# Layer 1's feed-forward norm: one pass over four batches, or each batch behind its own end

## The chip, the cores and the metric

The kernel runs on one core of a Trainium2 chip, as one program. The metric is the device time of one execution in microseconds (us). The core's engines work side by side, each through its own list of instructions in order: TensorE (PE in the profile: matrix products and transposes; PEld is its loading of weights), VectorE (DVE), ScalarE (ACT), GpSimd (POOL) and SyncE (SP). SP, ACT and POOL also start DMA transfers. An instruction that waits for a semaphore holds up everything behind it on its engine.

## The reference

A transformer of four layers works on x of 4 batches with 256 tokens of 256 features. Each layer is a cross attention (`xattn`) and a feed-forward part (`ffn`), both on a layer norm of x and both added to x. The stretch that matters is layer 1, between the end of layer 0's feed-forward and layer 1's experts:

```python
x = x + _L0_ffn_ref(_layernorm(x), ...)        # 32 experts, the best 8 of each token
x = x + _L1_xattn_ref(_layernorm(x), ...)
x = x + _L1_ffn_ref(_layernorm(x), ...)

def _L1_xattn_ref(Z, kv, ...):
    ...                                         # summary: one row of 256 for each batch, from kv alone
    y = Z + summary
    return (y - mu) / jnp.sqrt(var + LN_EPS) * gamma + beta

def _L1_ffn_ref(X, gate_w, router_bias, W1, W3, W2, sw1, sw3, sw2):
    scores = jax.nn.sigmoid(X @ gate_w.T)       # 8 experts
    _, idx = jax.lax.top_k(scores + router_bias, 2)
    ...
    y = jnp.einsum('eth,ehd->etd', jax.nn.silu(h1) * h3, W2)
    shared = (jax.nn.silu(X @ sw1.T) * (X @ sw3.T)) @ sw2.T
    return jnp.einsum('etd,te->td', y, gate_full) + shared
```

So layer 1's attention is for each batch a norm, an added row, a second norm, a scale and a shift: no matrix product on tokens. Its feed-forward part needs the third norm of the same batch, for the routing scores, for a shared expert that all tokens pass, and for the experts.

## The kernel before

A batch is one tile `x[b]` of [128, 2, 256]: token q*128+p lies in partition p. Everything is f32.

**Adding layer 0's experts (`l0_add`, L632 to L668).** For each of 8 token tiles t, GpSimd issues eight indirect gathers `f0yt` (L655), one for each of the eight chosen experts, into a ring of 24 buffers; two tiles later VectorE adds them to x (L647, eight instructions, whose order against each other is pinned). After every second tile a batch is whole, and `l1_xattn(b)` (L1303) runs on it: layer norm to y, plus the summary (L1308), layer norm to z, gamma (L1312), beta (L1313), added to x (L1314). All of this is VectorE's, save the roots of the norms, which ScalarE takes.

**Work for later in between (`fill`, L178).** Beside this, TensorE makes keys and values of the context for layer 2. That is a generator, `l2_early` (L1316); `fill(n)` takes n steps of it. A unit of it has 7 product steps (L1351: four matmuls 128x256 into PSUM, names `fill`, `filly`, `fillg`, `fillt` by buffer, copied by ScalarE to `kr_early`, L1358, and `va_early`, L1359, with squares, L1369, and sums of them on VectorE, L1370), a scaling of `kr_early` (L1376, by the engine in `self.scaler`) and 4 turn steps (L1385: transposes, copied by ScalarE to `kT_early`, L1387). `l0_add` takes `G0 = 9` steps for each t. What is left of the generator when layer 2 begins is taken there, at once.

**Layer 1's feed-forward (`l1_ffn`, L800).** It begins with `normed` (L188), which for each of the four batches in turn makes a layer norm `xn` (L152 to L163: stats L156, aggregate L157, root L125, reciprocal L126, scaled and shifted L160), stores it to DRAM as `f1xd` from ScalarE's queue (L195), takes `F1 = [1, 2, 2, 3]` steps of `fill`, turns it with four transposes `tp_ln` (L202) and copies them to `xnT` by turns on VectorE (L112) and ScalarE (L114). Then come 16 small products for the routing logits, the sigmoid (`l_sc`, L878), the choice of two experts (`first`, `l_sel` on), a table of slots, gathers from `f1xd`, and 23 expert tiles with `G1` fill steps between them. Beside the routing runs `shared_expert`, a generator of steps: each computes two pairs of products `f1gu` of a token tile, silu of one half on ScalarE (L831), times the other half on VectorE (L832), transposes `f1tps` and products `f1y`. All `f1gu`, the logits too, share two PSUM buffers.

**Order.** A scheduler places the instructions of each engine by their estimated readiness; `pin` (and `ordered`) fix one instruction's place behind the pinned one before it on the same engine. So lines of the program can change place against each other unless they are pinned or depend on each other. ScalarE's functions live in tables: root, sigmoid and silu are in different ones, and an `ACT_TABLE_LOAD` stands in its list wherever the next function needs another.

Of the kernel before, what the change touches and what calls it, by code (L numbers as in the profile page):

```python
# [11 lines left out]
F32 = mybir.dt.float32  # L12
# [6 lines left out]
AF = mybir.ActivationFunctionType  # L19
# [5 lines left out]
P = 128  # L25
B = 4
S = 256
NT = B * S
D = 256
# [10 lines left out]
E1, I1, SH1, K1 = 8, 176, 352, 2  # L40
# [7 lines left out]
F0 = [0, 0, 0, 0, 2, 12, 4, 4]  # L48
G0 = 9
REGS = 4  # L50
F1 = [1, 2, 2, 3]
G1 = [7, 4, 4, 3, 2, 2, 2, 2, 2, 2, 0]
LN2, Q2, C2 = 2, 2, 6
FIRST3 = [7, 1, 3]
# [43 lines left out]
class Kernel:  # L98
# [47 lines left out]
            if k < 2:  # L146
                yield 0.9

    def layernorm(self, out, x):

        nc = self.nc
        st = self.small.tile([P, 2, 6], F32, name="ln_st")  # L152
        mv = self.small.tile([P, 2, 2], F32, name="ln_mv")
        rs = self.small.tile([P, 2], F32, name="ln_rs")
        for q in range(2):
            nc.vector.bn_stats(st[:, q, :], x[:, q, :])  # L156
            nc.vector.bn_aggr(mv[:, q, :], st[:, q, :])  # L157
        self.rstd(rs, mv[:, :, 1], 1.0, self.eps5)
        for q in range(2):
            nc.vector.tensor_scalar(  # L160
                out[:, q, :], x[:, q, :], mv[:, q, 0:1], rs[:, q : q + 1],
                ALU.subtract, ALU.mult,
            )  # L163
# [469 lines left out]
    def l0_add(self, two, weights):  # L633


        nc = self.nc
        slot, gate, yd = self.back0
        self.scaler = nc.vector
        take = self.take
        self.take = self.wide_take  # L640
        rows = []

        def add(t):
            xt = self.x[t // 2][:, t % 2, :]
            for r in range(K0):
                self.pin(
                    nc.vector.scalar_tensor_tensor(xt, rows.pop(0), gate[:, t, r : r + 1], xt, ALU.mult, ALU.add)  # L647
                )
            if t % 2:
                self.l1_xattn(t // 2)  # L650

        for t in range(9):
            for r in range(K0 if t < 8 else 0):
                yt = two.tile([P, D], F32, name="f0yt", bufs=3 * K0)
                nc.gpsimd.indirect_dma_start(  # L655
                    out=yt, out_offset=None, in_=yd[:, :],
                    in_offset=bass.IndirectOffsetOnAxis(ap=slot[:, t, r : r + 1], axis=0),
                )
                rows.append(yt)
            if t > 1:  # L660
                add(t - 2)
            self.fill(G0)
            if t > 5:
                next(weights, None)
        add(7)
        self.idle(self.take()[:, :D], self.y1[:, 0, :], 4)
        self.scaler = nc.gpsimd
        self.take = take  # L668
# [128 lines left out]
    def l1_ffn(self, weights):  # L797
# [7 lines left out]
        nc, tc = self.nc, self.tc  # L805
# [3 lines left out]
        with ExitStack() as es:  # L809
            one = es.enter_context(tc.tile_pool(name="f1one", bufs=1))  # L810
            two = es.enter_context(tc.tile_pool(name="f1two", bufs=2))
            ps, ps_g, ps_y = self.psf
            s13, s2, w13, w2 = self.w1f
            for _ in weights:
                pass
            xd = self.dram.tile([NT, D], F32, name="f1xd")
            yd = self.dram.tile([NS * P, D], F32, name="f1yd")

            slot = one.tile([P, K1, 8], U32, name="f1slot")
# [2 lines left out]
            ei = one.tile([1, NS], U32, name="f1ei")  # L822
            rt = es.enter_context(tc.tile_pool(name="f1r", bufs=1))
            low, keep, lane, tok = self.low, self.keep[:, :E1], self.lane, self.tok
            xT = self.normed(ps, F1[:B], xd, rt)

            def gated(gu, w, x, h):

                for k in range(2):
                    self.mm(gu, x(k), w(k), k == 0, k == 1)  # L830
                nc.scalar.activation(h, gu[:, :I1], AF.Silu)  # L831
                nc.vector.tensor_tensor(h, h, gu[:, I1:], ALU.mult)  # L832

            def products():
                return ps_g.tile([P, 512], F32, name="f1gu", tag="gu")

            def shared_expert():

                last = None
                for t in range(9):  # L840
                    now = None
                    if t < 8:
                        h = two.tile([P, SH1], F32, name="f1hs")
                        for c in range(2):
                            gated(
                                products()[:, : 2 * I1], lambda k: s13[:, c, k, :],
                                lambda k: xT[t // 4][:, k, (t % 4) * P : (t % 4 + 1) * P], h[:, c * I1 : (c + 1) * I1],
                            )
                        now = (t, h)
                    if last is not None:  # L850
                        u, h = last
                        tp = ps.tile([P, 3, P], F32, name="f1tps", tag="tp")
                        hT = two.tile([P, 3, P], F32, name="f1hTs")
                        y = ps_y.tile([P, 512], F32, name="f1y", tag="y")[:, :D]
                        for m in range(3):
                            n = min(P, SH1 - m * P)
                            nc.tensor.transpose(tp[:n, m, :], h[:, m * P : m * P + n], self.ident)
                        nc.scalar.copy(hT[:, :2, :], tp[:, :2, :])
                        nc.scalar.copy(hT[:n, 2, :], tp[:n, 2, :])
                        for m in range(3):  # L860
                            n = min(P, SH1 - m * P)
                            self.mm(y, hT[:n, m, :], s2[:n, m, :], m == 0, m == 2)
                        xt = self.x[u // 2][:, u % 2, :]
                        nc.vector.tensor_tensor(xt, xt, y, ALU.add)
                    last = now
                    yield

            shared = shared_expert()
            beside = lambda n: [next(shared, None) for _ in range(n)]

# [42 lines left out]
            for n in range(NS):  # L913
                t = two.tile([P, D], F32, name="f1xr", bufs=4)
                nc.gpsimd.indirect_dma_start(
                    out=t, out_offset=None, in_=xd[:, :],
# [39 lines left out]
            def through(n):  # L956
                h = two.tile([P, I1], F32, name="f1h", bufs=3)
                gated(
                    products()[:, : 2 * I1], lambda k: w13[:, bass.ds(expert[n], 1), k, :],
                    lambda k: xsT[n][:, k, :], h,  # L960
                )
                return h
# [32 lines left out]
            for t in range(11):  # L995
                for r in range(K1 if t < 8 else 0):
                    yt = two.tile([P, D], F32, name="f1yt", bufs=4 * K1)
                    nc.gpsimd.indirect_dma_start(
                        out=yt, out_offset=None, in_=yd[:, :],
# [304 lines left out]
    def l1_xattn(self, b):  # L1304
        nc, one, rows = self.nc, self.a1, self.rows1
        y = one.tile([P, 2, D], F32, name="y1", bufs=2)
        self.layernorm(y, self.x[b])
        nc.vector.tensor_tensor(y, y, self.summary[b][:, None, :].to_broadcast([P, 2, D]), ALU.add)  # L1308
        self.y1 = y
        z = one.tile([P, 2, D], F32, name="z1", bufs=2)  # L1310
        self.layernorm(z, y)
        nc.vector.tensor_tensor(z, z, rows["l1_gamma"][:, None, :].to_broadcast([P, 2, D]), ALU.mult)  # L1312
        nc.vector.tensor_tensor(z, z, rows["l1_beta"][:, None, :].to_broadcast([P, 2, D]), ALU.add)  # L1313
        nc.vector.tensor_tensor(self.x[b], self.x[b], z, ALU.add)  # L1314

    def l2_early(self, ctxT):  # L1316

# [1347 lines left out]
```

## Time and profile before

| | |
|---|---|
| time, median of 3 runs | 2369.67 us (2365.74 to 2370.74) |
| the profiled execution | 2363.93 us |
| its span (first to last instruction) | 2362.2 us |
| mean granted TensorE clock | 0.981 |
| `l0_add` in the span | about 372 to 504 us |
| layer 1's feed-forward up to the first expert tile | about 504 to 552 us |
| its expert tiles | about 552 to 640 us |

PE is busy 96% of the whole span and DVE 62%, but these shares average over stages with different limits; the stretch of the change is read by windows. A row of the profile's groups has the line, the engine, the operation, `out<-in` by the names above with partitions x elements, then how often, busy time and the mean of one. These are the norm's and the turn's operations on VectorE from 457 to 520 us:

```profile
L156 DVE BATCH_NORM_STATS2 ln_st<-x 128x6 f32<-128x256 f32 x12 | 4.8, 408 | 0.0
L157 DVE BATCH_NORM_AGGREGATE ln_mv<-ln_st 128x2 f32<-128x6 f32 x18 | 2.9, 169 | 0.1
L160 DVE TENSOR_SCALAR xn<-x,ln_mv,ln_rs 128x256 f32<-128x256 f32 x8 | 2.8, 404 | 0.2
L112 DVE COPY xnT<-tp_ln 128x512 f32<-128x512 f32 x2 | 1.4, 693 | 1.5 <-PE tp_ln L202 1.5
```

The first line reads: twelve instructions of L156, 4.8 us in all, 408 ns each, with no idle time of VectorE ahead of them. In the last, 1.5 us of idle time lay ahead of the two copies, ended by the transposes. Lines of a timeline begin with the start in the span and the length; what stands in brackets is the idle time of that engine just before and what ended it.

### The profile page before, as it was taken

To read this page: it belongs to the slowest core of one execution; us is meant where nothing else is said; L and a number is where in the kernel's file an instruction comes from. 1 tells how busy PE (TensorE), PEld (TensorE's weight loads), DVE (VectorE), ACT (ScalarE), POOL (GpSimd) and SP (SyncE) were. 2 spreads that over 40 slices of the span, in tenths; PEclk is the share of its full clock that TensorE was granted. 3 is DMA by queue.
4 is the path that set the end of the run, shared out by engine and by line. 5 is a ranking of instruction groups with operands and counts; after the bars stand their busy time and mean duration, and the time that the engine had idled before them with its cause. 6 is when DMAs were issued, how large, how long until landed. Compare 5 with 4: busy or idle time off the path is not lost.

```text
span 2362.2 us, 42374 instructions
## 1 busy us (share of the span) xinstructions
PE 2256.3 (96%) x14395; PEld 1383.5 (59%) x14395; DVE 1464.7 (62%) x3534; ACT 1271.0 (54%) x2884; POOL 944.4 (40%) x1716
## 2 busy tenths in 40 slices
PE   8999997889989999999999999999999989999998
PEld 5677876767745555555555565555765633343332
DVE  5553532783557777877787777877434484748343
ACT  3334443552474555555555555554332488888996
POOL 2015655503345544555545555444212253424220
PEclk9999998999999999999999999999899999999999
DMA  7165575652551111111111111100434354434320
GB/s 270 42 203 175 173 152 157 198 182 72 166 179 40 36 51 46 53 52 51 52 56 51 52 43 51 43 24 10 193 126 114 89 169 120 107 100 104 81 68 18
DMA packets 157166, 234.47 MB, mean 99 GB/s; under 512 B 33993, under 2 KB 122825, under 8 KB 155754
## 3 DMA queue, kind: packets, MB, share of 16 engines
q1 hardware_dynamic: 140902, 190.86, 25.1%
q0 software_dynamic: 11280, 31.60, 5.4%
q10 hardware_dynamic: 4772, 9.31, 1.3%
q8 instruction: 118, 1.93, 0.3%
q14 instruction: 94, 0.77, 0.1%
HBM read 169.94 MB, written 61.74 MB: 98 GB/s over the span
## 4 chain that ended last, share of the span: by engine, by line
PE 80%; DVE 8%; DMA 3%; issue 3%; ACT 2%; POOL 2%; SPq 0%; ACTq 0%; DVEq 0%; another core or an unknown queue 0%; POOLq 0%
PE o L117 18%; PE s L117 17%; PE o L77 7%; PE b L77 4%; PE f2gu L117 3%; PE s L77 3%; PE fill L1351 3%; PE acc L117 2%; PE f1gu L117 2%; PE tpq L117 2%; PE f0gu L117 2%; PE av L117 2%; DMA f0xr<-f0xd,f0src 2%; PE f0y L117 1%; PE f2y L117 1%
## 5 line engine op out<-in xcount | busy, mean ns | idle before, releaser
L1616 ACT ACTIVATE p<-s,nmsm 128x448 f32<-128x448 f32 (+2 forms) x512 | 324.4, 638 | 388.3 <-DVE nmsm L1611 316.8
L117 PE MATMUL o<-pT,va 128*128 128x256 f32 (+2 forms) x1920 | 431.7, 377 | 0.4 <-DVE pT L1660 0.3
L117 PE MATMUL s<-kT,qT 128*32 128x448 f32 (+2 forms) x4096 | 424.2, 550 | 4.2 <-ACT p L1616 4.2
L77 ACT ACTIVATE e<-s 128x1024 f32<-128x1024 f32 (+1 forms) x416 | 392.9, 1040 | 54.3 <-PE s L77 53.1
L117 PEld LDWEIGHTS o<-pT,va 128*128 128x128 f32 (+1 forms) x1920 | 344.8, 190 | 124.7 <-issue 72.5
L1654 POOL TENSOR_SCALAR p<-p,rm 128x416 f32<-128x416 f32 x508 | 317.0, 645 | 6.3
L1611 DVE TENSOR_REDUCE nmsm<-s 128x1 f32<-128x448 f32 (+4 forms) x384 | 293.1, 784 | 4.2
L1660 DVE STREAM_TRANSPOSE pT<-p 128x448 f32<-128x448 f32 (+4 forms) x384 | 278.0, 779 | 9.9 <-POOL p L1654 9.9
L117 PEld LDWEIGHTS s<-kT,qT 128*32 128x32 f32 x4096 | 121.7, 110 | 250.1 <-issue 213.8
L77 PE MATMUL o<-e,va 128*32 128x512 f32 (+1 forms) x1664 | 248.4, 610 | 5.4 <-DVE os L77 5.2
L1644 POOL TENSOR_TENSOR rm<-em,tot 32x8 f32<-32x8 f32 x256 | 49.9, 195 | 337.1 <-DVE tot L1641 304.7
L1608 DVE TENSOR_TENSOR s<-s,mask 128x64 f32<-128x64 f32 (+4 forms) x384 | 92.3, 260 | 125.0 <-PE s L117 74.9
L77 PEld LDWEIGHTS s<-qb,kb 32*128 32x128 f32 (+1 forms) x1664 | 65.4, 181 | 175.0 <-issue 131.0
L545 POOL DMA_INDIRECT f0xr<-f0xd,f0src x95 | 90.9, 957 | 65.6 <-PE f0y L117 25.4
L1351 PE MATMUL fill<-wkc_early,ctxT 128*128 128x256 f32 (+1 forms) x444 | 107.7, 395 | 9.3 <-ACT va_early L1359 8.5
L77 PE MATMUL s<-qb,kb 32*128 32x256 f32 (+1 forms) x1664 | 111.3, 331 | 2.9 <-ACT e L77 1.3
L1616 ACT ACTIVATION_READ_ACCUMULATOR p<-s,nmsm 128x1 f32 x512 | 100.5, 196 | 0.0
L1351 PEld LDWEIGHTS fill<-wkc_early,ctxT 128*128 128x128 f32 (+1 forms) x444 | 85.6, 196 | 25.4 <-ACT va_early L1359 10.2
L77 POOL CAST kb<-kf 128x384 fp32r<-128x384 f32 (+1 forms) x126 | 64.4, 540 | 89.7 <-PE s L77 31.2
L655 POOL DMA_INDIRECT f0yt<-f0yd,f0slot x64 | 63.0, 985 | 60.6 <-DVE x L647 29.8
L1370 DVE TENSOR_REDUCE ss_early<-sq_early 128x4 f32<-128x512 f32 x64 | 37.1, 580 | 79.7 <-ACT sq_early L1369 56.1
L117 PE MATMUL f2gu<-f2wgu,f2xsT 128*128 x176 | 84.6, 605 | 0.6 <-ACT f2xsT L114 0.3
(569 smaller groups left out, 3688.1 us busy)
## 6 DMA issues: line engine op xcount, KB each, us to landing
kf<-kd SPq DMA_DIRECT2D x384, 48.0 KB
vd<-va_early SPq DMA_DIRECT2D x96, 128.0 KB
kd<-kT_early SPq DMA_DIRECT2D x48, 256.0 KB
kT<-kd SPq DMA_DIRECT2D x16, 768.0 KB
va<-vd SPq DMA_DIRECT2D x16, 768.0 KB
kd<-kt SPq DMA_DIRECT2D x96, 128.0 KB
f0yd<-f0ys SPq DMA_DIRECT2D x95, 128.0 KB
ctxT<-in_ctxT SPq DMA_DIRECT2D x5, 1664.0 KB
```

The source lines that it names most:

```text
L77: ins = f(*a, **kw)
L117: self.ordered(self.nc.tensor.matmul(out, lhsT, rhs, start=start, stop=stop, **kw))
L545: nc.gpsimd.indirect_dma_start(out=t, out_offset=None, in_=xd[:, :], in_offset=bass.IndirectOffsetOnAxis(ap=src[:, n : n + 1], axis=0),)
L655: nc.gpsimd.indirect_dma_start(out=yt, out_offset=None, in_=yd[:, :], in_offset=bass.IndirectOffsetOnAxis(ap=slot[:, t, r : r + 1], axis=0),)
L1351: ins = nc.tensor.matmul(tp[:rows, t, :], ctxT[u // NKV2][:, k, c0 : c0 + rows], w[u % NKV2][:, k, :], start=k == 0, stop=k == 1,)
L1370: nc.vector.tensor_reduce(ss[:, m0:m1], sq[:, : m1 - m0, :], AX.X, ALU.add)
L1608: nc.vector.tensor_tensor(sv, sv, mask[:, e0:e1, : nt - CT, :].rearrange("p n t i -> p n (t i)"), ALU.add)
L1611: nc.vector.tensor_reduce(ms[:, 0, e0:e1], s[:, n0:n1, : nt * 32], AX.X, ALU.max, negate=True)
L1616: nc.scalar.activation(p[:, n, : nt * 32], s[:, n, : nt * 32], AF.Exp, bias=ms[:, 0, e : e + 1], accum_out=ms[:, 1, e : e + 1],)
L1644: nc.gpsimd.tensor_tensor(r[32 * a : 32 * a + 32], e[:, a], tot, ALU.mult)
L1654: nc.gpsimd.tensor_scalar(p[:, n, : nt * 32], p[:, n, : nt * 32], r[:, e : e + 1], 1.0, ALU.mult, ALU.mult)
L1660: self.pin(nc.vector.transpose(pT[:, 2 * c + n0 : 2 * c + n1, :nt, :].rearrange("p n t i -> p n (t i)"), p[:, n0:n1, : nt * 32],))
```

## The change

The norm and the turn of `normed` become two methods, `norm1(b)` and `turn1(b)`, for layer 1's feed-forward. For batches 0, 1 and 2 they are called in `l0_add`, at t = 3, 5 and 7, directly behind the adds and the attention that end the batch: the norm ahead of that tile's nine fill steps, the turn behind them. The last batch's stay in `l1_ffn`, with all of `F1`, now 5 steps instead of 8 in all, between them. `xn` comes from a pool of two buffers instead of four of its own. The norm's root is written out, and the last batch's is pinned, as is the silu of the first token tile in the shared expert. `normed` itself stays for the other layers.

```diff
-F1 = [1, 2, 2, 3]
+F1 = 5
...
-    def layernorm(self, out, x):
+    def layernorm(self, out, x, held=False):
...
-        self.rstd(rs, mv[:, :, 1], 1.0, self.eps5)
+        ins = nc.scalar.activation(rs, mv[:, :, 1], AF.Sqrt, bias=self.eps5, scale=1.0)
+        if held:
+            self.pin(ins)
+        nc.vector.reciprocal(rs, rs)
...
             if t > 1:
                 add(t - 2)
+            if t in (3, 5, 7):
+                self.norm1(t // 2 - 1)
             self.fill(G0)
+            if t in (3, 5, 7):
+                self.turn1(t // 2 - 1)
...
-            xd = self.dram.tile([NT, D], F32, name="f1xd")
+            xd, xT = self.xd1, self.xT1
...
-            xT = self.normed(ps, F1[:B], xd, rt)
-
-            def gated(gu, w, x, h):
+            self.norm1(B - 1)
+            self.fill(F1)
+            self.turn1(B - 1)
+
+            def gated(gu, w, x, h, held=False):
...
-                nc.scalar.activation(h, gu[:, :I1], AF.Silu)
+                ins = nc.scalar.activation(h, gu[:, :I1], AF.Silu)
+                if held:
+                    self.pin(ins)
...
-                                lambda k: xT[t // 4][:, k, (t % 4) * P : (t % 4 + 1) * P], h[:, c * I1 : (c + 1) * I1],
+                                lambda k: xT[t // 4][:, k, (t % 4) * P : (t % 4 + 1) * P], h[:, c * I1 : (c + 1) * I1], not t,
...
+    def norm1(self, b):
+
+        if not b:
+            self.xd1 = self.dram.tile([NT, D], F32, name="f1xd")
+            self.xT1 = [self.xnT.tile([P, 2, 512], F32, name=f"xnT{tb}", tag="xnT") for tb in range(2)]
+        self.xn1 = self.xn.tile([P, 2, D], F32, name="xn")
+        self.layernorm(self.xn1, self.x[b], b == B - 1)
+        self.nc.scalar.dma_start(self.xd1.rearrange("(b q p) d -> b p q d", p=P, q=2)[b], self.xn1)
+
+    def turn1(self, b):
+        tp = self.psf[0].tile([P, 2, 2, P], F32, name="tp_ln", tag="tp")
+        for k in range(2):
+            for q in range(2):
+                self.nc.tensor.transpose(tp[:, k, q, :], self.xn1[:, q, k * P : (k + 1) * P], self.ident)
+        o = (b % 2) * S
+        self.evac(self.xT1[b // 2][:, :, o : o + S], tp.rearrange("p k q t -> p k (q t)"))
```

In the order that the scheduler makes of it, the first batch's four transposes stand behind 23 matmuls of a unit's products, ahead of the rest of them; the second's and third's stand inside later units in the same way. All five steps of `F1` stand ahead of the matmuls on y with which `l0_add` ends (L666: TensorE multiplies y by a unit matrix, into a buffer that nothing reads). Behind these come the logits of six token tiles, one product pair of the shared expert, the last batch's transposes and the logits of the last two tiles. ScalarE's list has two table loads in this stretch instead of five, and four scalings of `kr_early` go from GpSimd to VectorE.

## The prediction

> **What bounds the kernel now.** A change of this kernel can be told from none at about 0.2%, 4.7 us. The profiled execution took 2363.9 us (span 2362.2 and 1.7 around it), 5.7 below the median of 2369.7; terms are read in its time and the difference is applied to the median.
>
> I read the windows first (columns: from:to, length, then busy time and instruction count of PE, PEld, DVE, ACT, POOL, then PE clock, DMA share, GB/s).
>
> ```profile
> 442.00:454.00 12.00, 3.68 (x10) 1.80 (x10) 3.37 (x8) 1.52 (x5) 6.87 (x8) 0.74 0.59 205
> 457.00:475.00 18.00, 18.00 (x88) 15.74 (x88) 17.34 (x43) 11.13 (x34) 8.73 (x8) 0.97 0.65 202
> 475.00:490.00 15.00, 12.58 (x64) 10.45 (x63) 14.18 (x36) 9.56 (x30) 0.00 (x0) 1.00 0.61 208
> 498.00:504.00 6.00, 4.95 (x18) 3.81 (x18) 5.83 (x21) 2.06 (x6) 0.00 (x0) 0.72 0.10 30
> 512.00:516.00 4.00, 4.00 (x16) 2.79 (x16) 1.25 (x5) 1.63 (x3) 2.90 (x3) 0.58 0.94 266
> 526.00:552.00 26.00, 25.29 (x125) 18.77 (x124) 12.12 (x47) 6.32 (x22) 4.25 (x5) 1.00 0.07 21
> 552.00:608.00 56.00, 55.76 (x268) 42.25 (x267) 19.98 (x54) 16.94 (x56) 17.50 (x19) 1.00 0.31 91
> ```
>
> Three regimes. From 442 to 454 nothing is busy: PE does 3.68 us of 12. From 457 to 504 DVE sets the pace (17.34 of 18, 14.18 of 15, 5.83 of 6). From 512 to 608 PE is full. The change works across all three. Then the chain of waits (start, length, what) between the last batch's end and the routing:
>
> ```profile
> 506.39 0.70 DVE xnT L112
> 507.14 3.13 PE f1gu L117 x20
> 510.81 0.70 DVE xnT L112
> 511.56 3.48 PE f1gu L117 x12
> 517.73 1.28 ACT L878
> 519.02 0.23 ACT l_sc L878
> 519.28 0.24 DVE l_sel L881
> ```
>
> Each batch's copy is waited for by its logits, with a product pair of the shared expert between, and the scores `l_sc` come 15.4 us after the last add into x ends (503.86). Last ScalarE's timeline there, and what PE waited for from 457 to 523:
>
> ```profile
> 508.61 1.28 ACT L831 ACT_TABLE_LOAD   x1
> 510.24 1.28 ACT L125 ACT_TABLE_LOAD   x1
> 512.05 1.28 ACT L831 ACT_TABLE_LOAD   x1
> ...
> PE fill L1351 <- ACT va_early L1359: 2.0, 1, 2.0
> PE fillg L117 <- DVE y L1308: 1.9, 1, 1.9
> ```
>
> The fourth batch's root (ended 511.83) stands behind two table loads, because a gate function got between it and the third's. PE's waits (total, times, longest) are slack that DVE's pace leaves.
>
> **The tail, from y of the last batch on (gain).** Before, DVE finishes y (L1308) at 498.40, the last add (L1314) at 503.86, and PE has all logits and three product pairs behind it at 518.1 (eight r products from 517.19, 0.95). I call that point S. After:
> - DVE now carries batch 1's and 2's norms before y. One norm is two bn_stats (0.75 together), the last aggregate 0.16, reciprocal 0.17, two xn 0.73: 1.8 us. Batch 2's copy is on DVE too (0.69). 2 x 1.8 + 0.69 = 4.3; DVE idles about 1 us in that stretch (0.24, 0.39, 0.36), so between 3.3 and 4.3; I take 3.5: y at 501.9.
> - The end of the last batch took 5.46 us with four foreign bn_stats and their aggregates in between (about 0.36 each by the starts): without them 4.0, so the last add ends at 505.9.
> - Last norm: stats 0.92, root 0.29 and 0.1 of hop, reciprocal and hop 0.25, xn 0.73: 2.2, to 508.1. Transposes 0.45, copy 0.7 with hops 0.04: 509.3. Four r products of the last two tiles, 0.12 each: 509.8. The sigmoid's table load follows ScalarE's last work, 509.3 + 1.28, then 0.23: `l_sc` at 510.8 against 519.25.
> - Product pairs: one is ordered before the last transposes. There are two PSUM buffers, one holding the logits, so the second pair (four matmuls, 1.43 in the row at 508.06) starts when the sigmoid is done, to 512.3; the third waits for the first pair's silu (510.8 + load 1.28 + 0.32) and product 0.33, 512.8, and ends at 514.3. So S moves from 518.1 to 514.3: **-3.8**. After S PE is full in both (25.29 of 26, 55.76 of 56), and DVE's routing chain is earlier by more than PE's work, so it doesn't decide. Bounds: -1.7 (the idle PE time 504 to 520 alone: 0.34 + 0.25 + 0.35 + 0.79) to -5.4 (second and third pair directly behind the logits: 509.8 + 2 x 1.43 = 512.7).
>
> The Trainium skill, "ScalarE: Activation LUTs", section "What ACT_TABLE_LOAD costs", gives about 1.28 us for the load plus a drain of about 1.38, 2.66 for a switch. The trace has the 1.28 but lets the sigmoid start 0.01 after its load. As S stands behind two switches now, the page's price would put it 2.8 later and leave -1.0 of the gain. I keep to the row.
>
> **Three fill steps moved out (cost later).** The early stream gives 5 steps in this stage instead of 8; G1's counts are the same, so three steps fall due at the start of layer 2. A step is a product step (1.73) or a turn step (0.44, the last 0.11): between 1.0 and 5.2, mean 3.45. PE is idle there for 4.03 us at 645.47 (waiting for `va_early`), which may take them whole; uncovered they cost all. Between 0 and +5.2; I take **+1.0**, nearest to the idle row.
>
> **The first batch's turn, placed among products (cost).** PE gets the four `tp_ln` after 23 matmuls of a unit, where it stands at 427.45 before. Batch 0's x ends on DVE at 429.54, and its norm with `kr_early` scalings (0.6 each) in between is ready near 432.7. PE waits 5.2 us; behind it are the unit's other products, then ScalarE's `kr_early` and `va_early` copies that read them. ScalarE itself stops at the store of xn(0) on its queue, with the copies behind. Cover: PE's idle 2.04 + 0.39 + 1.87 = 4.3 us from 484 to 498, where DVE is the pace. Cost between 0 and +0.9 (5.2 - 4.3) if that cover holds, +5.2 without; I take **0**, since DVE is ready no earlier than 501.9.
>
> **The gathers behind it (unknown).** DVE's copy of batch 0 waits for that turn, so the second batch's adds start near 433.9 instead of 430.26, and their release of `f0yt` buffers lets GpSimd's next gathers go.
>
> ```profile
> 431.01 0.94 POOL L655 DMA_INDIRECT f0yt<-f0yd,f0slot  x1 [4.11 <-DVE x L647]
> ...
> 450.05 0.95 POOL L655 DMA_INDIRECT f0yt<-f0yd,f0slot  x1 [0.31 <-issue]
> 442.85 1.64 issue
> 444.87 1.75 issue
> 447.00 1.74 issue
> ```
>
> Sixteen gathers run unbroken from 431.0 to 451.0, and eleven us into them PE, waiting for nothing that the profile shows, falls to one instruction in 1.7 us or so, until 453.6 (chain, "issue"). At 371.7 to 394 it is the same; the eights at 402.9 and 416.9 show none. What ties them the trace doesn't say. If the stall goes with the burst, it moves 3.6 us later at most: +3.6; if not, 0; if the burst breaks in two eights, about 8 us of PE come free (12 - 3.68): -8. DVE idles 8.5 us in one wait there, room for delayed adds, so I take **+1.0**.
>
> **Small parts.** Root and reciprocal written out are the same two operations: 0. The four `kr_early` scalings that go from GpSimd (3.39) to DVE (4 x 0.6) lie under 526 to 552, DVE 12.12 of 26: 0; uncovered, 2.4. The xn stores (issue 0.37 on ScalarE's queue) are needed only by the expert gathers behind the routing (541.8): 0. SP's and GpSimd's queues are passed by nothing else.
>
> **Sum:** -3.8 + 1.0 + 0 + 1.0 = -1.8 us: 2363.9 to 2362.1, and 2369.7 to **2367.9**. Its ends together are -5.4 (2364.3) and -1.7 + 5.2 + 0.9 + 3.6 = +8.0 (2377.7); as not all of them come at once, the forecast's own range is 2364 to 2373.
>
> **Rivals.**
> - *The gather burst is broken and PE's starvation shrinks* (0.28). For: eights show no stall, and the release is now split by the copy. Against: the adds behind it are bunched, not spread. -2.8 - 8 with part given back in DVE's stretch (it must do the added 4.3): about 2359.
> - *The turn costs in place and its cover is gone* (0.22), slower. Starvation follows the burst (+3.6) and PE enters it 5.2 us behind, with no idle left from 484 to 498 because PE, not DVE, is then late: -2.8 + 3.6 + 5.2 = +6.0, 2375.7. It decides once PE's delay passes 4.3 us. For: DVE's 8.5 us wait was already for work that PE feeds. Against: DVE grows by 4.3 in the same stretch.
> - *The norm work is only pushed along* (0.10): S moves by the 1.7 of idle time, the moved fills cost it again: 2369.
>
> **Chances.** The forecast has 0.40, of which 0.09 beyond -4.7 and 0.01 beyond +4.7. Faster 0.28 + 0.09 = 0.37; slower 0.22 + 0.01 = 0.23; same 0.40. The range reaches into the two outer cases, 2357 to 2377: below it lies a starvation that goes almost whole (0.08), above it a turn that costs more than its 5.2 (0.08).
>
> **What would show it.** Right: two table loads between 503 and 520; `l_sc` within 6 us of the last add; PE's wait for xn near 427 of about 5 us and none for `va_early` at 484; y near 502; S near 514. Wrong: `issue` rows that end before 450 or after 457; PE waiting for the first `gated` buffers over 2 us; or layer 2's first `s` product over 2 us later, counted from the last expert tile.

## The result, and the profile after

The changed kernel is slower: 2377.92 us median (2373.09 to 2382.84, 7 runs) against 2366.25 (2358.92 to 2370.74, 7 runs) beside it, a ratio of 1.0049 with a 95% interval of 1.0034 to 1.0064, so 8 to 15 us. The forecast was 2367.9, in a range of 2357 to 2377.

The profiled execution of after took a span of 2379.3 us, of before 2362.2. Not all of these 17 us are the change's: the first gather of `l0_add` starts at 372.98 instead of 364.21, and up to there both kernels run the same instructions. So everything below is read in segments, from one instruction's start to another's.

After's windows over the stretch (columns as in the prediction):

```profile
442.00:460.00 18.00, 18.00 (x84) 15.29 (x85) 10.40 (x23) 8.40 (x25) 8.36 (x9) 0.91 0.78 259
460.00:480.00 20.00, 12.66 (x47) 9.83 (x46) 17.36 (x48) 7.18 (x21) 15.73 (x15) 0.75 0.47 138
480.00:500.00 20.00, 18.94 (x98) 16.30 (x96) 15.78 (x40) 14.41 (x41) 1.60 (x2) 0.99 0.78 256
500.00:520.00 20.00, 18.10 (x91) 15.54 (x91) 17.89 (x46) 9.39 (x26) 0.00 (x0) 1.00 0.56 182
520.00:540.00 20.00, 17.40 (x73) 11.54 (x73) 8.97 (x49) 6.64 (x15) 0.00 (x0) 0.83 0.49 140
```

The hole of before at 442 to 454 is gone. There is a new one at 460 to 480 (PE 12.66 of 20). From 520 to 540, behind the last add, PE is neither full nor at full clock (17.40, 0.83). That alone is no loss: the stage lies some 18 us earlier in before, and was much the same there:

```profile
500.00:520.00 20.00, 18.27 (x91) 13.96 (x90) 12.28 (x49) 11.32 (x22) 3.39 (x4) 0.86 0.73 236
```

What PE of after waited for from 430 to 540 (total, times, longest):

```profile
PE tp_ln L1340 <- DVE xn L163: 11.5, 4, 5.2
PE filly L1379 <- ACT va_early L1387: 2.0, 1, 2.0
PE fill L1379 <- ACT va_early L1387: 1.3, 2, 1.0
```

The transposes `tp_ln` wait for the norm at all four batches. PE's timeline shows the first two, with the idle time ahead in brackets:

```profile
441.90 0.87 PE L1340 MATMUL tp_ln<-ident,xn 128*128 128x128 f32 x4 [4.05 <-DVE xn L163]
442.60 3.45 PE L1379 MATMUL fillt<-wkc_early,ctxT 128*128 128x256 f32 x8
...
475.85 1.22 PE L1340 MATMUL tp_ln<-ident,xn 128*128 128x128 f32 x4 [5.19 <-DVE xn L163]
476.87 1.06 PE L1413 MATMUL fillt<-ident,kr_early 128*128 128x128 f32 x4
```

4.05 us at the first, 5.19 at the second; the eight products behind the first take 3.45 where a later row of eight (448.73) takes 1.89, as the clock has fallen meanwhile (0.60 granted from 443 to 447). Last, after's tail, first on ScalarE, then on PE:

```profile
525.50 1.28 ACT L889 ACT_TABLE_LOAD   x1
526.80 0.22 ACT L889 ACTIVATE l_sc<-f1gu 128x64 f32<-128x64 f32 x1
527.04 1.28 ACT L840 ACT_TABLE_LOAD   x1
528.34 0.32 ACT L840 ACTIVATE f1hs<-f1gu 128x176 f32<-128x176 f32 x1
```

```profile
527.08 1.74 PE L117 MATMUL f1gu<-l_s,xnT 128*128 128x352 f32 x4 [0.48 <-ACT l_sc L889]
529.64 5.06 PE L117 MATMUL f1gu<-l_s,xnT 128*128 128x352 f32 x8 [0.82 <-DVE f1hs L843]
```

Two table loads instead of five, and the scores 5.55 us behind the last add (521.25) instead of 15.8: that part does what it says. But silu comes only behind the sigmoid, the product pairs wait for it, and eight of their matmuls take 5.06 us, at a granted clock of 0.50 from 530 to 534. In before the three pairs there took this long, the middle one at a low clock too (0.58 from 512 to 516):

```profile
508.06 1.43 PE L117 MATMUL f1gu<-l_s,xnT 128*128 128x352 f32 x4
...
512.47 2.57 PE L117 MATMUL f1gu<-l_s,xnT 128*128 128x352 f32 x4
...
515.90 1.46 PE L117 MATMUL f1gu<-l_s,xnT 128*128 128x352 f32 x4
```

Segments of every profile, in us; the kernels below `after_again` are explained with the experiments. Batch 1, 2, 3: from the last add (L1314 in before) of one batch to that of the next. Tail: from the last batch's to `f1src`, the table that the expert gathers wait for. Layer 2: from the last expert's silu to the first score product (between the two lie 65.8 us that are the same in all).

| kernel | batch 1 | batch 2 | batch 3 | tail | layer 2 | time against before |
|---|---|---|---|---|---|---|
| before, first profile | 33.5 | 21.1 | 19.8 | 38.7 | 74.1 | |
| before_again | 33.0 | 21.1 | 19.8 | 36.3 | 74.1 | |
| after | 33.7 | 25.8 | 23.4 | 35.9 | 75.6 | 1.0049 (1.0034 to 1.0064) |
| after_again | 33.9 | 26.7 | 23.4 | 36.4 | 75.7 | 1.0049 (1.0036 to 1.0062) |
| nosilu | 33.5 | 26.0 | 23.4 | 32.1 | 75.7 | 1.0023 (1.0008 to 1.0038) |
| later_nosilu | 33.2 | 25.0 | 21.3 | 34.7 | 75.7 | 1.0018 (1.0008 to 1.0028) |
| *without the stall:* before_3 | 23.5 | 21.1 | 19.8 | 38.5 | 70.7 | |
| turn_later | 23.7 | 23.6 | 19.3 | 37.3 | 73.5 | 1.0018 (1.0005 to 1.0031) |
| turns_end | 24.6 | 23.9 | 18.5 | 35.8 | 73.8 | 1.0028 (1.0014 to 1.0041) |
| pins_only | 23.5 | 21.1 | 19.8 | 42.4 | 71.7 | 1.0019 (1.0006 to 1.0032) |
| fill8 | 28.2 | 25.7 | 24.7 | 35.2 | 70.3 | 1.0044 (1.0027 to 1.0062) |
| nosilu_2 | 27.9 | 26.1 | 23.4 | 32.1 | 73.2 | 1.0034 (1.0022 to 1.0046) |
| end_nosilu | 24.6 | 23.9 | 20.0 | 33.3 | 73.5 | 0.9994 (0.9983 to 1.0005) |
| end8_nosilu | 24.6 | 23.9 | 21.9 | 32.2 | 70.9 | 0.9999 (0.9989 to 1.0009) |
| two_nosilu | 24.6 | 23.9 | 17.6 | 34.7 | 71.7 | 0.9998 (0.9987 to 1.0010) |
| before5 | 23.6 | 21.1 | 19.8 | 38.1 | 73.1 | 1.0009 (0.9997 to 1.0021) |
| pool_before | 23.5 | 19.5 | 22.5 | 40.1 | 69.5 | 0.9995 (0.9985 to 1.0004) |
| pool_end | 24.6 | 25.4 | 19.9 | 39.6 | 72.6 | 1.0028 (1.0015 to 1.0041) |

One thing has to be known for the lower rows: in these groups of runs TensorE had none of its unexplained stall, in any kernel, and before took 2317 to 2320 us instead of 2366. Ratios are always against before in the same group.

After_again against before_again, part by part: +0.9, +5.6, +3.6, +0.1 and +1.6, together 11.8 us; the ratio says 11.6. The loss is in batches 2 and 3, and the tail gives nothing back. In the first pair the batches lose about as much (+0.2, +4.7, +3.6), but the tail is 2.8 us shorter. Before's own tail varies with the clock: 36.3 us where it was 1.00 all through (before_again), 38.7 and 38.5 where it averaged 0.96 (before and before_3).

### The profile page after: what moved, and what is told of

Its sections match the earlier page's. It is cut to its first block, busy times and chain, and to the rows that moved or that the text cites. A ratio compares the mean times of both kernels' runs of the same rounds, so it can differ in the third digit from the quotient of the medians.

```text
span 2379.3 us, 42325 instructions
## 1 busy us (share of the span) xinstructions
PE 2264.2 (95%) x14381; PEld 1390.4 (58%) x14395; DVE 1466.5 (62%) x3538; ACT 1268.6 (53%) x2881; POOL 947.1 (40%) x1712
## 4 chain that ended last, share of the span: by engine, by line
PE 81%; DVE 9%; issue 3%; DMA 3%; ACT 2%; POOL 1%; SPq 0%; another core or an unknown queue 0%; ACTq 0%; DVEq 0%; PEldq 0%; POOLq 0%
PE o L117 18%; PE s L117 16%; PE o L77 7%; PE b L77 4%; PE f2gu L117 3%; PE s L77 3%; PE fill L1379 3%; PE acc L117 2%; PE f0gu L117 2%; PE tpq L117 2%; PE f1gu L117 2%; PE av L117 2%; PE f0y L117 2%; PE f2y L117 1%; DMA f0xr<-f0xd,f0src 1%
## 5 line engine op out<-in xcount | busy, mean ns | idle before, releaser
L1379 PE MATMUL fill<-wkc_early,ctxT 128*128 128x256 f32 (+1 forms) x464 | 117.1, 408 | 7.4 <-ACT va_early L1387 5.2
L1379 PEld LDWEIGHTS fill<-wkc_early,ctxT 128*128 128x128 f32 (+1 forms) x464 | 93.3, 204 | 25.3 <-ACT va_early L1387 6.9
```

The source lines that it names most:

```text
L1379: ins = nc.tensor.matmul(tp[:rows, t, :], ctxT[u // NKV2][:, k, c0 : c0 + rows], w[u % NKV2][:, k, :], start=k == 0, stop=k == 1,)
```

## The experiments

The theory after the result: **A**, PE's in-order wait at the early turns is the loss. **B**, VectorE's added norms are, wherever the turns stand. Others: the pins (D), the fill steps moved to layer 2 (E), or luck ahead of the stretch (C).

### First group: the turns later, the turns at the end, the pins alone, eight steps

`turn_later`:

```diff
             self.fill(G0)
-            if t in (3, 5, 7):
-                self.turn1(t // 2 - 1)
+            if t in (4, 6, 8):
+                self.turn1(t // 2 - 2)
```

> The changed kernel with the three early turns one token tile later, behind that tile's fill steps (t = 4, 6, 8 instead of 3, 5, 7). Theory A (PE's in-order wait at the early turns sets the loss: 4.05 + 5.19 + 1.69 us of wait for xn, products at half clock behind it): the waits for xn at the turns fall from 11.5 us in all to under 4, and the time by 6 to 10, to 2368 to 2372. Rival B (VectorE's added norms in the stretch that it paces, 1.8 us for each batch, are the loss wherever the turn stands): 2375 to 2380, the last add into x no earlier than now. Rival C (the difference lies ahead of the stretch, in a clock that happened to be low): no change against the changed kernel, and the stretch ahead of the gathers shows it.

`turns_end`:

```diff
             self.fill(G0)
-            if t in (3, 5, 7):
-                self.turn1(t // 2 - 1)
...
+            for b in range(B - 1):
+                self.turn1(b)
             self.norm1(B - 1)
...
-        self.xn1 = self.xn.tile([P, 2, D], F32, name="xn")
+        self.xn1 = self.xn1s[b] = self.y1 if b == 2 else self.xn.tile([P, 2, D], F32, name="xn")
```

> The changed kernel with the norms where they are and the three early turns at the start of the feed-forward part (the third norm is written over y of its batch, which nothing else reads by then). No turn stands among the products of the early stream any more. Theory A: no wait of PE for xn before 500 us, time 2364 to 2370. Rival B: the norms still lengthen VectorE's stretch by about 4 us: 2374 to 2379. Rival C: as the changed kernel, 2378.

`pins_only` is before, with:

```diff
-            self.layernorm(xn, self.x[b])
+            self.layernorm(xn, self.x[b], bool(pool) and b == B - 1)
...
-                nc.scalar.activation(h, gu[:, :I1], AF.Silu)
+                ins = nc.scalar.activation(h, gu[:, :I1], AF.Silu)
+                if held:
+                    self.pin(ins)
```

> The kernel before with the two pins alone: the last batch's root and the first token tile's silu in program order; no norm and no turn moves. Theory A and rival B both put the loss into the moved norms and turns, so the pins cost nothing: 2362 to 2367, with two or three table loads instead of five between the last add and the scores. If the pins themselves are the loss (rival D: product pairs wait for a silu that stands behind the sigmoid, with two buffers of PSUM), 2370 or more.

`fill8`:

```diff
-F1 = 5
+F1 = 8
```

> The changed kernel with eight fill steps in the feed-forward part as before, instead of five. If the three steps that fall due at layer 2's start are what is lost (rival E), the time falls by 3 to 5 us, to 2373 to 2375. Theory A: those steps only move, 2376 to 2380, and layer 2's first score product is as much earlier as the routing is later.

Before took 2317.42 us in this group, so the absolute times that were expected have no meaning here; the ratios do. fill8 has the eight steps back and still loses 0.44%, close to after's 0.49% in the group with the stall: the loss doesn't need the moved steps (E), nor luck ahead of the stretch in one group (C). turn_later and turns_end lose 0.18% and 0.28%, well under fill8. PE's waits for xn from 400 to 475 fell to one of 2.9 in turn_later:

```profile
PE tp_ln L1340 <- DVE xn L163: 2.9, 1, 2.9
```

In turns_end one of 2.08 is left, before the third turn at 454.39; the profile calls it `issue`, but VectorE begins to write that norm only at 453.90. Batches 1 to 3 together are 66.5 and 67.0 us against fill8's 78.7. So A holds for the batches, and B is left with a few us of them. But both should then have come near before, and did not. The reason is in pins_only, against what A and B said: it loses 0.19%, 4.4 us, without any moved norm. Its segments are those of before up to the last add, and its tail is 42.4 us. PE there, by timeline and windows:

```profile
475.59 1.88 PE L117 MATMUL f1gu<-r,xnT 128*128 128x8 f32 x8 [0.68 <-ACT xnT L114]
477.78 7.03 PE L117 MATMUL f1gu<-l_s,xnT 128*128 128x352 f32 x12 [0.31 <-ACT l_sc L883]
```

```profile
470.00:474.00 4.00, 3.32 (x25) 2.77 (x24) 2.79 (x13) 0.67 (x3) 0.42 (x1) 0.98 1.04 393
474.00:478.00 4.00, 3.01 (x13) 2.52 (x14) 0.23 (x1) 2.35 (x4) 2.97 (x4) 0.50 0.94 256
478.00:482.00 4.00, 4.00 (x7) 2.11 (x8) 3.07 (x30) 1.66 (x3) 0.00 (x0) 0.50 0.71 176
```

The pinned silu stands behind the sigmoid on ScalarE, so the product pairs that used to run between the batches' logits wait. PE has only the logits' small products and transposes left, with gaps of up to 0.68 between; the granted clock falls to 0.50 at 474 and stays there while the twelve matmuls that were held back run: 7.03 us, where twelve at the 1.43 of four would take at most 4.3. This is rival D, and it is in after too. Over the 10 us from the scores on, the clock averages 0.66 to 0.83 in all six profiles with the pin and 1.00 in all twelve without it. So the pin costs clock there. Why the clock falls isn't settled: before lost some as well, ahead of its scores, in two of its three profiles (0.89 on average from the last add to the scores) and none, with the same list, in the third (before_again).

The Trainium skill ("TensorE: Matmul & The Clock Gate", section "What's actually happening") lets the clock fall to half after an idle window of about 3.4 us. Here it fell although PE was busy 3.32 of the 4 us before by the profile, and in nosilu below it stayed at 1.00 with 3.59 of 5; the measured rows decide.

### Second group: both kernels again, and the pin taken out

`nosilu` (and `nosilu_2`, the same kernel in the last group) and `later_nosilu`, which has turn_later's edit as well:

```diff
-                                lambda k: xT[t // 4][:, k, (t % 4) * P : (t % 4 + 1) * P], h[:, c * I1 : (c + 1) * I1], not t,
+                                lambda k: xT[t // 4][:, k, (t % 4) * P : (t % 4 + 1) * P], h[:, c * I1 : (c + 1) * I1],
```

> The kernel before once more, for its profile on the chip of this group. In the first four experiments, on another chip than the profile of before, the stall of TensorE with nothing to wait for (in 442 to 454 us of the first profile) was not there. If it belongs to the chip, its absence here goes with a time near 2317 and no such stall in this profile; if it belongs to the kernel before, the stall is here again whatever the time.

> The changed kernel on the same chip. Theory A (turns) with the pin of the silu added: waits of PE for xn at the early turns of 8 to 12 us in all, and a low clock behind the scores; 9 to 13 us above before. If the first comparison was carried by the stall of TensorE on its chip, the two kernels differ by less than 5 us on a chip without the stall.

> The changed kernel without the pin on the first token tile's silu (the root's pin stays). With the pin alone, the kernel before took 12 products in 7.03 us at a clock of 0.50 behind the scores. If the pin does that in the changed kernel as well, from the last add into x to f1src shortens from 35.9 to 32 to 34 us and the time falls by 2 to 4 us, with five table loads back. If the earlier logits already hide it, no change: within 1.5 us of the changed kernel.

> Both causes taken out: the three early turns one token tile later, and no pin on the silu. If the turns and the pin are the whole loss, the rest of the change is worth what was forecast, and the time is at or below before: -3 to +1 us against it. If VectorE's added norms cost by themselves, it stays 2 to 5 us above before.

The stall is there again in this group, and before takes 2366.8. After_again repeats the first result to the digit (1.0049); its waits for xn are 12.6 us. nosilu halves the loss to 0.23%: its tail is 32.1 us instead of 36.4. Its last pairs (timeline of PE) run between the logits again, at full clock:

```profile
517.39 1.45 PE L117 MATMUL f1gu<-l_s,xnT 128*128 128x352 f32 x4 [0.78 <-DVE f1hs L843]
...
520.63 1.45 PE L117 MATMUL f1gu<-l_s,xnT 128*128 128x352 f32 x4 [0.20 <-DVE f1hs L843]
521.92 0.95 PE L117 MATMUL f1gu<-r,xnT 128*128 128x8 f32 x8
```

So the silu's pin (the root's stays in nosilu) costs 4.3 us of tail (the ratios differ by a little more, 0.26% or 6 us), and that is all that early norms had gained in the tail (36.3 to 32.1). The scores come later without it (9.26 us behind the last add instead of 5.91), and `f1src` earlier: how soon the scores are there decided nothing, PE's work up to the routing did.

later_nosilu was a miss: 0.18%, not at or under before. Its batches 2 and 3 are still 5.4 us over before's (46.3 against 40.9). PE waits 4.4 us at the third turn there, and early norms with late turns cost 3.0 in these two batches (end_nosilu below). Part of TensorE's stall is back too, but in batch 1, where before has it (`issue` waits from 455 to 461). One tile later is not late enough.

### Third group: no early turn, no pin

`end_nosilu` is turns_end with nosilu's edit. `end8_nosilu` has `F1 = 8` besides. `two_nosilu` has the third batch's norm back in the feed-forward part:

```diff
-            if t in (3, 5, 7):
+            if t in (3, 5):
                 self.norm1(t // 2 - 1)
...
-            for b in range(B - 1):
+            for b in range(2):
                 self.turn1(b)
+            self.norm1(2)
+            self.fill(2)
+            self.turn1(2)
             self.norm1(B - 1)
-            self.fill(F1)
+            self.fill(F1 - 2)
```

`before5` is before with `F1 = [1, 1, 1, 2]`.

> The changed kernel with the three early turns at the start of the feed-forward part (third norm written over y of its batch) and no pin on the silu: early norms and five fill steps are what is left of the change. On the chip without the stall, early turns cost 8 us between the ends of batches 1 and 3 and early norms alone 1.5 to 2; without the pin the stretch from the scores to f1src is 22.8 instead of 30.4 us. Expected: from the last add to f1src 32 to 33 us against 36.3 of before, the two batches 42 to 43 against 40.9, layer 2's start 1.5 to 2 later: in all 0 to 3 us under before. If the norms are the loss as well: 2 to 5 above.

> The same with eight fill steps in the feed-forward part, as before. If the three moved steps cost at layer 2's start what they save here, the same time as with five, within 1.5 us; if layer 2's idle time took them, 2 to 3.5 us slower than with five.

> As the first of this group, but only two batches have their norm early; the third's norm and turn are in the feed-forward part with two fill steps behind it. VectorE's stretch gets 1.8 us less, the tail one turn and one copy more. If VectorE's pace decides: 1 to 2 us under the version with three; if TensorE's in-order tail decides: 0 to 2 above it.

> The kernel before with five fill steps (1, 1, 1, 2) in the feed-forward part instead of eight, and nothing else. The step of the forecast that charged 1.0 us for them at layer 2's start and counted 3.45 as gained in the stage says: 1 to 3 us under before. If the three steps are TensorE's cover for the waits for norms and copies there, their gap opens: from the last add to f1src no shorter, and 0 to 3 us above before.

With the turns and the pin gone the loss is gone: 0.9994. Against nosilu_2 the turns alone make 68.5 us out of 77.3 in the three batches, 8.9 us, and 0.40% of the time (0.9994 against 1.0034). A and D account for the whole loss. The copies of the turns and their transposes are no part of it: in end_nosilu they too stand ahead of the last batch's end (450 to 459, that end at 472.08), and only their place differs. What differs on VectorE from the end of batch 0 to that of batch 3: it waits 6.1 us for squares of the early stream in nosilu_2 and 1.4 in end_nosilu, and 1.5 us for the turns' transposes against none, together 6.2 of the 8.9. But nothing is won either. Eight steps or five (0.9999 and 0.9994) and two early norms or three (0.9998) are within each other's intervals. before5 shows why five bring nothing: its tail is 0.5 us shorter than before_3's and its layer 2 starts 2.4 us later. It is unclear as a time (0.9997 to 1.0021), and its mean is on the losing side.

### Fourth group: where the tail's gain goes

`pool_before` and `pool_end` (on end_nosilu):

```diff
             if t > 1:
                 add(t - 2)
+            if t == 7:
+                self.scaler = nc.gpsimd
```

> Early norms, turns at the start of the feed-forward part, no pin on the silu, and from t = 7 on GpSimd scales kr_early instead of VectorE (two units, 2.1 us of VectorE each, GpSimd has nothing after its last gather). If VectorE's added norms are what repays the tail, its stretch shortens by 2 to 4 us and the time is 2 to 4 us under before. If another engine sets the pace there, the same as before within 1.5 us.

> The kernel before with that move to GpSimd alone. VectorE's pace: 2 to 4 us under before, as much as it brings beside the early norms. If it brings something only together with them: no change.

> The changed kernel without the silu's pin again, beside the others of this group. Theory A: 5 to 9 us above before, and more on a chip without the stall (where the first turn has no stall to stand in) than the 0.23% of the other chip.

> The kernel before, for its profile beside this group. Without the stall: from the end of batch 1 to that of batch 3 40.9 us, from there to f1src 36 to 38.

before_3 has no stall, and 40.9 us for the batches as expected; the rest is 38.5, where 36 to 38 was expected. Against it, end_nosilu gains 5.3 us in the tail (the mean clock there is 0.95 and 0.96), and pays 1.2, 2.8 and 0.2 in the batches and 2.8 at layer 2's start: +1.7 in these profiles, -1.4 in the medians, nothing that can be told. That is where the gain goes. New in the batches are VectorE's three norms and the three turns, of which only the third still waits for its norm (written from 455.36 on):

```profile
455.86 0.30 PE L1341 MATMUL tp_ln<-ident,y 128*128 128x128 f32 x1 [2.07 <-issue]
```

The counter-test failed: taking two units' scalings off VectorE didn't bring it out. pool_before is at 0.9995: batch 2 gets 1.6 us shorter, batch 3 2.7 longer. pool_end is slower than end_nosilu, 1.0028. PE then waits for the scaling:

```profile
PE filly L1416 <- POOL kr_early L1407: 1.8, 1, 1.8
```

and its tail is 39.6 instead of 33.3. So the test moved the wait to GpSimd instead of relieving VectorE, and whether VectorE's time alone repays the tail stays open; the segments show where it is repaid, not that VectorE's busy time is the cause. nosilu_2 came as expected (0.34%): without the stall batch 1 is 3.3 us longer with the first turn in it (27.9 against end_nosilu's 24.6), though PE waits only 0.94 there; in the group with the stall it was 0.5 longer than before's (33.5 against 33.0).

No version was found that beats before by more than the runs can tell.

## Why the prediction was wrong, point by point

**The turn (the step that failed most).** The forecast worked out one turn, the first, at 5.2 us of waiting and took 0 for it, since PE's idle time from 484 to 498 was to cover it. The wait was there (4.05), and batch 1 grew by no more than 0.2 and 0.9 us, but not through that cover, which lies two batches later. Most likely it was because TensorE's stall, which stands in that batch in before (8 to 9 us of `issue` waits), was not there in after. That no cost showed was luck. The second and third turns stand among products in the same way, as the list of the changed order said, and were priced only as norm work on VectorE. They waited 5.19 and 1.69 us, in after_again 6.88 and 1.68, at a place that has no cover: PE feeds the squares and scalings that VectorE's next batch stands in line with (the 6.2 us of waits above). Batches 2 and 3 grew by 9.2 us (after_again), of which the early norms, with the turns out of the way, make 3.0 (end_nosilu against before_3).

**The product pairs behind the scores.** The forecast let the second and third pair wait for the sigmoid and the silu, and counted 1.43 for a pair. The wait was right, the size was not: the clock fell to half, and eight matmuls took 5.06. The timeline of before already had a pair of 2.57 (at 512.47) beside the 1.43, and the forecast's own window from 512 to 516 a clock of 0.58, which it read only as PE being full. It put S 8.4 us behind the end of the last add; measured it is 10.4 (the first four of the eight end at 532.35, the last add at 521.94). Before had 14.2, or 12.0 at full clock (before_again). Without the pin the pairs don't wait and the tail is 4.3 us shorter. That the pin alone could lose time was not among the rivals.

**The last norm to the scores.** 4.9 us were worked out, from the end of the last add to the end of `l_sc`; 5.1 (after) and 5.4 (after_again) were measured: right, and worth nothing by itself. That a function starts at once behind its table load, to which the forecast kept, held too (a load of 1.28 from 525.50, the sigmoid at 526.80).

**VectorE's norms.** +2.0 us for the last add, measured +4.2 over three batches where the turns are late (end_nosilu), 3.0 of it in batches 2 and 3, which the forecast's term was for. Right in kind, too small in size.

**The moved fill steps.** +1.0 at layer 2, between 0 and 5.2: measured +1.6 in after and +2.4 in before5. The idle time that was to take them shrank, but a new wait came. PE's waits at layer 2's start in after:

```profile
PE fill L1379 <- ACT va_early L1387: 1.7, 1, 1.7
PE tp_ln L1497 <- ACT kT_early L1415: 1.7, 1, 1.7
```

4.0 us of `va_early` in before have become 1.7, and 1.7 for `kT_early` are new: the steps fill one gap and the layer's first transposes stand behind them. In the groups without the stall there is less of a gap to fill: before_3 waits only 1.4 us for `va_early` there.

**The gathers.** +1.0 taken; to the end of batch 1 it is +0.2 and +0.9 in the two pairs of profiles. That holds the first norm and turn and the lost stall as well, so the agreement says nothing of the gathers. A burst of gathers alone doesn't bring the stall: in before_3 all 64 go out unbroken and none follows.

**The rivals.** The slower one had the mechanism ("the turn costs in place and its cover is gone"), but the wrong turn for it, and TensorE's stall, which it added, had no part in it; that its 2375.7 comes near the median of 2377.9 is luck. It was given 0.22. The faster one (0.28) saw its condition come true: in after the sixteen gathers that went out unbroken are parted by 5.35 us (eight from 444.2, the next from 459.4), and no stall stands in batch 1. Yet the batch is no shorter (33.7 us against 33.5).

## What to carry to other kernels

Work that an engine takes in order between other work costs by when its input is ready, once for every place where it stands: price each copy of a moved step at its own place, not the first for all. When a scheduler is told an order by hand, look at what used to run in the gap that it closes; here a pin that saved three table loads took products out of the gaps of TensorE, and its clock was low when they ran. An earlier result is worth only what the engine that sets the pace behind it does less.

## What the runs showed of the hardware

The same program took 2317 us in some groups of runs and 2366 in others, and one of the chips ran a group of each kind. The difference lies in TensorE's stall. Windows of before_again and of before_3, at the first gathers:

```profile
380.00:390.00 10.00, 2.90 (x7) 1.48 (x7) 2.67 (x6) 2.57 (x5) 7.62 (x8) 0.69 0.53 157
390.00:400.00 10.00, 2.65 (x5) 1.14 (x4) 0.00 (x0) 1.05 (x2) 5.68 (x6) 0.50 0.41 125
```

```profile
377.00:390.00 13.00, 13.00 (x68) 11.45 (x67) 9.23 (x21) 8.27 (x24) 9.95 (x11) 1.00 0.83 249
390.00:400.00 10.00, 10.00 (x54) 8.83 (x53) 8.89 (x24) 6.77 (x20) 7.72 (x8) 1.00 0.73 217
```

In the first, PE issues 12 matmuls in 20 us and waits for nothing that the profile names (24.1 us of `issue` in all from 370 to 460); in the second it is full. From the first gather to the end of batch 1 that is 97.5 us against 62.7, 34.8 of the 43.9 between the two spans. What makes it come and go was not found. It matters for reading the table: the same change lengthened batch 1 by 0.2 to 0.9 us where before has the stall in it, and by 4.4 where there is none (nosilu_2 against before_3).
